# Neighbour lists from a dense adjacency: keys formed in SBUF by VectorE, or in PSUM by ScalarE and TensorE

## The chip, the cores and the metric

The kernel runs on one core of a Trainium2 chip. The core has five engines, each with a queue of its own that it works through in order: PE (TensorE, matrix products), DVE (VectorE), ACT (ScalarE), POOL (GpSimd) and SP, which here only starts transfers. They share SBUF; PE writes its products to PSUM[...], which DVE and ACT can also read and write. The time is device microseconds of one execution, the median of some runs; the profile is of one further execution. Line numbers in the profile of the kernel before are those of its source.

## The reference

A stack of four graph layers on x (8 x 2048 x 64), all masked by one 2048 x 2048 adjacency of zeros and ones with 8249 ones. The rows are uneven: the densest has 91, most have only a few. Cut to what matters here:

```
h = relu(layernorm(x));  x = x + softmax(where(adj > 0, h h^T / 8, -1e12)) h          # layer 0
h = relu(layernorm(x));  x = x + elu(softmax(where(adj > 0, lrelu(f1 + f2), -9e15)) hW) # layer 1
h = relu(layernorm(x));  x = x + layernorm(attention of 4 heads and of their output)    # layer 2, mask adj + I
h = relu(layernorm(x));  x = x + relu(softmax(where(adj > 0, lrelu(f1 + f2), -1e12)) hW) # layer 3
```

A row without any edge gets the mean over all nodes, which is why every layer's table carries one extra row, the column mean.

## The kernel before, in words

The 2048 nodes are 16 blocks of 128 rows, one row per partition; a node's row holds all eight batches, 512 values. Since the adjacency is sparse, the kernel doesn't compute 2048 x 2048 scores. It makes, once, a list of neighbours for each node, and every layer then gathers neighbour rows from a table in memory by indirect DMA (`gather`, L259). Block i has `ROWS[i]` list columns that all its nodes use, and `PACKED[i]` columns in which longer lists of different nodes are packed together, with selection matrices `sel` and `selt` (128 x 128) that copy a query to its packed edges and sum them back.

The lists are made in `lists` (L621), from a block's 128 x 2048 adjacency rows in int32, loaded by `load_adj` in one transfer of 1 MB, two buffers. In order:

- L626, DVE: key = (a > 0) * (2049 - column), in place in the tile `a`, read afterwards as float32. `keyrow` holds 2049 - column for all partitions.
- L632: the row is cut into segments, narrow at the left where the columns are dense, wide at the right; in each, MAX8 takes the eight largest keys into the candidate tile `c`. `SEGS` gives 8 segments and one round for blocks 2 to 15, 16 and one for block 1, 24 and two for block 0. Where there are two rounds, MATCH_REPLACE8 (L634) zeroes the eight found, in place, before the second MAX8.
- L642 and L644: of the candidates, the largest 16 (blocks 4 to 15), 24 (1 to 3) or 128 (block 0), again by MAX8 and MATCH_REPLACE8 in turn.
- L646 to L708: indices, masks, degrees, a running sum of degrees by a triangle matmul on PE (L661), the selection matrices (ACT L678, DVE L679, PE transposes L684, ACT L685), and the packed columns' indices (PE L696, DVE L698 to L708).

L637, L646 and L665 record whether a segment, a list or the packed columns overflowed. If one did, a flag makes a dense version of the whole stack run behind; the last lines of `edge_stack` compute that flag.

`pipeline` (L218) runs its stages over the blocks in the order of `MAKING` (15, 14, 13, 0, 12, 11, 10, 1, ...), each stage one block behind the stage ahead of it. Two pipelines make up this part (L710 to L712). The first normalizes x for layer 0: DVE sums (L276, L288), ACT squares (L290), DVE sums (L296, L297), POOL takes the power -1/2 (L299, L301), ACT scales (L307), SP stores the rows in the table, and POOL adds them up in `acc`; behind the last block PE sums `acc` over partitions (L371), DVE copies the mean row (L374) and SP stores it. The second runs load_adj, lists, gather, scores and exponents (`first0`), weighted sums (`second`), division and residual (`third0`), and the norm and table of layer 1, ending with that layer's mean row. Gathers of a layer can begin only when its whole table and mean row are stored.

The order of each engine's queue isn't written by hand. A scheduler takes the instructions of both pipelines, with their dependences, and puts each engine's into one fixed order when the kernel is built, by its own estimate of when each can start; tiles are handed out from pools with a fixed number of buffers. `ps_q` has three PSUM banks (tile `q`), used by the queries of the scores (L428, L437), the selection matrices and the transposes; `ps_m` and `ps_y` have two each, and one bank holds small tiles.

Of the kernel before, what the change touches and what calls it, by code (L numbers as in the profile page):

```python
# [7 lines left out]

F32 = mybir.dt.float32
F16 = mybir.dt.float16  # L10
I32 = mybir.dt.int32
U8 = mybir.dt.uint8
AF = mybir.ActivationFunctionType
OP = mybir.AluOpType
AX = mybir.AxisListType

P = 128
# [5 lines left out]
U16 = mybir.dt.uint16  # L23
# [6 lines left out]
PACKED = [8, 2, 3, 3, 2, 1, 2, 1, 1, 1, 1, 2, 2, 1, 1, 1]  # L30
WIDTH = [128, 24, 24, 24] + [16] * 12
SEGS = [(24, 2), (16, 1)] + [(8, 1)] * 14
RING = 26
TEMP = 16.0

# [11 lines left out]

def segments(n, count, least):

    ends, lo = [], 0  # L50
    for k in range(1, count + 1):
        hi = n * k * k // (count * count)
        if hi - lo >= least:
            ends.append((lo, hi))
            lo = hi
    if lo < n:
        ends[-1] = (ends[-1][0], n)
    return ends


# [1 line left out]
def edge_stack(ctx: ExitStack, tc: tile.TileContext, x_in, adj, w1, w1t, a1, wh, wht, bh, wo, bo,  # L62
# [9 lines left out]
    nc = tc.nc  # L72
    N, F = x_in.shape
# [13 lines left out]
    ident = const.tile([P, P], F32, name="ident")  # L87
# [15 lines left out]
    most2 = const.tile([P, NT], F32, name="most2")  # L103
    ring = const.tile([P, RING, F + B], F32, name="g")
    qidx = const.tile([P, sum(PACKED)], I32, name="qidx")
# [44 lines left out]
    with tc.tile_pool(name="setup", bufs=1) as sp, \  # L150
# [25 lines left out]
        for h in range(H):  # L176
            p = ps_w.tile([P, D], F32, name="p")
            nc.tensor.matmul(p, wh2[:, h].rearrange("d t c -> d (t c)"), wh2[:, h, 0, :],
                             start=True, stop=True)
# [57 lines left out]

    def rows(i, lo, hi, most=RING):

        t = lo  # L240
        while t < hi:
            at = (held[i] + t) % RING
            m = min(most, hi - t, RING - at)
            yield t, m, ring[:, at:at + m, :]
            t += m

    def row(i, t):
        return ring[:, (held[i] + t) % RING, :F]

    taken = {}  # L250

    def gather(k, i, st, behind=None):

        n = SLOTS[i]
        assert sum(SLOTS[j] for j in held) + n <= RING
        held[i], front[0] = front[0], (front[0] + n) % RING
# [332 lines left out]
    with tc.tile_pool(name="rows", bufs=2) as rp:  # L589
        rows_pool[0] = rp  # L590
        sel_all[0] = rp.tile([P, sum(PACKED) * P], F32, name="sel", bufs=1)
        with tc.tile_pool(name="lists", bufs=2) as pool, \
                tc.tile_pool(name="ps_q", bufs=3, space=bass.MemoryType.PSUM) as ps_q, \
                tc.tile_pool(name="ps_t", bufs=1, space=bass.MemoryType.PSUM) as ps_t:
            bank[0] = ps_t.tile([P, F], F32, name="tiny")
            keyrow = pool.tile([P, N], U16, name="keyrow", bufs=1)
            nc.gpsimd.iota(keyrow, pattern=[[-1, N]], base=N + 1, channel_multiplier=0,
                           allow_small_or_imprecise_dtypes=True)
            LS = 512
            iota = pool.tile([P, LS], F32, name="iota", bufs=1)  # L600
            nc.gpsimd.iota(iota, pattern=[[1, LS]], base=0, channel_multiplier=0,
                           allow_small_or_imprecise_dtypes=True)
# [3 lines left out]
                           allow_small_or_imprecise_dtypes=True)  # L606
            pe = pool.tile([P, NT], F32, name="pe", bufs=1)
            nc.gpsimd.iota(pe, pattern=[[P, NT]], base=0, channel_multiplier=1,
                           allow_small_or_imprecise_dtypes=True)
# [5 lines left out]
                                    pattern=[[1, P]], channel_multiplier=-1)  # L615

            def load_adj(i, st):
                st["a"] = pool.tile([P, N], I32, name="a")
                nc.sync.dma_start(out=st["a"], in_=adj[i * P:(i + 1) * P, :])

            def lists(i, st):  # L621

                K, T, W = ROWS[i], PACKED[i], WIDTH[i]
                E = T * P
                key = st["a"].bitcast(F32)
                nc.vector.scalar_tensor_tensor(key, st["a"], 0.0, keyrow, op0=OP.is_gt, op1=OP.mult)  # L626
                count, rounds = SEGS[i]
                segs = segments(N, count, 8 * rounds)
                c1 = pool.tile([P, len(segs), rounds, 8], F32, name=f"c{i}" if i < 2 else "c", bufs=1)
                for s, (lo, hi) in enumerate(segs):  # L630
                    for r in range(rounds):
                        nc.vector.max(out=c1[:, s, r, :], in_=key[:, lo:hi])  # L632
                        if r < rounds - 1:
                            nc.vector.match_replace(out=key[:, lo:hi], in_to_replace=c1[:, s, r, :],  # L634
                                                    in_values=key[:, lo:hi], imm_value=0.0)
                full = [s for s, (lo, hi) in enumerate(segs) if hi - lo > 8 * rounds]
                nc.vector.tensor_reduce(over[:, i, 0:1], c1[:, full[0]:, rounds - 1, 7:8].rearrange("p s o -> p (s o)"),  # L637
                                        AX.X, OP.max)
# [2 lines left out]
                for r in range(W // 8):  # L641
                    nc.vector.max(out=ell[:, 8 * r:8 * r + 8], in_=flat)  # L642
                    if r < W // 8 - 1:
                        nc.vector.match_replace(out=flat, in_to_replace=ell[:, 8 * r:8 * r + 8], in_values=flat,  # L644
                                                imm_value=0.0)
# [3 lines left out]
                at = OFF[i]  # L649
# [22 lines left out]
                mine = sel_all[0][:, POFF[i] * P:POFF[i] * P + E]  # L672
                for e0 in range(0, E, LS):
                    n = min(LS, E - e0)
                    if e0:
                        nc.vector.tensor_scalar(nmid, nmid, float(LS), None, op0=OP.add)
                    p = ps_q.tile([P, F], F32, name="q")
                    nc.scalar.activation(p[:, :n], iota[:, :n], AF.Abs, bias=nmid)  # L678
                    nc.vector.tensor_scalar(mine[:, e0:e0 + n], p[:, :n], half, None, op0=OP.is_lt)  # L679
                for t0 in range(0, T, 4):  # L680
                    n = min(4, T - t0)
                    p = ps_q.tile([P, F], F32, name="q")
# [8 lines left out]
                for t0 in range(0, T, step):  # L691
                    n = min(step, T - t0)
# [6 lines left out]
                    for t in range(n):  # L699
                        eq = pool.tile([P, P], F32, name="eq")  # L700
                        nc.vector.scalar_tensor_tensor(eq[:, :V], iotaj[:, :V], col[:, t:t + 1], pv[:, t, :V],
                                                       op0=OP.is_equal, op1=OP.mult,
                                                       accum_out=ke[:, t0 + t:t0 + t + 1])
                    nc.vector.tensor_scalar(qidx[:, POFF[i] + t0:POFF[i] + t0 + n], pv[:, :, V + 1], -1.0, N + 1.0,
                                            op0=OP.mult, op1=OP.add)
# [3 lines left out]

            pipeline(xin_rows, lambda i, st: norm_a(st["x"], st, False), pre_b, pre_c(None), pre_d(0, None))  # L710
            pipeline(load_adj, lists, take0, both(first0, xin_rows), second, third0, pre_b, pre_c(u1),
                     pre_d(1, u1))  # L712

# [148 lines left out]
    with psum_pools()[0] as ps_q, psum_pools()[1] as ps_t, tc.tile_pool(name="rows2", bufs=2) as rp:  # L862
# [72 lines left out]
        p = ps_m.tile([P, F], F32, name="m")  # L935
        nc.tensor.transpose(p[:1, :P], v[:, 3:4], ident)
        lo = small.tile([1, 1], F32, name="lo", bufs=1)
# [466 lines left out]
def whole_stack(tc, t, out):  # L1404
    nc = tc.nc
    D = t["gamma"].shape[0]
    with tc.tile_pool(name="flag", bufs=1) as pool:
        flag = pool.tile([1, 1], I32, name="flag")
        edge_stack(tc, t["x"], t["adj"], t["w1"], t["w1t"], t["a1"], t["wh"], t["wht"], t["bh"], t["wo"],
                   t["bo"], t["gamma"], t["beta"], t["w3"], t["w3t"], t["a3"], out, flag)  # L1410
        bad = nc.values_load(flag, min_val=0, max_val=1)
        with tc.If(bad > 0):
            gnn_stack(tc, t["x"].rearrange("n (b d) -> n b d", d=D), t["adj"], t["w1"], t["a1"], t["wht"],
                      t["bh"], t["wo"], t["bo"], t["gamma"], t["beta"], t["w3"], t["a3"],
                      out.rearrange("n (b d) -> n b d", d=D))
# [36 lines left out]
```

## Time and profile before

| | us |
|---|---|
| median of 3 runs | 1659.34 (1657.62 to 1660.49) |
| the profiled execution, first to last instruction | 1660.9 |
| layer 0's mean row, PE's sum of it (L371) | 106.06 to 107.92 |
| layer 1's mean row copied by DVE (L374) | 401.86 |
| first gather of layer 1 issued | 404.64 |

| over the whole execution | busy us | share | instructions |
|---|---|---|---|
| PE | 1214.6 | 73% | 3771 |
| DVE | 1311.9 | 79% | 2674 |
| ACT | 741.6 | 45% | 2362 |
| POOL | 1151.1 | 69% | 903 |

| lines of the lists on DVE | instructions | busy us |
|---|---|---|
| L626, forming the keys, 128 x 2048 | 16 | 38.7 (2418 ns each) |
| L632, MAX8 on the segments | 172 | 51.1 |
| L634, MATCH_REPLACE8 on segments, with its loads | 44 | 5.5 |
| L642, MAX8 on candidates | 49 | 15.7 |
| L644, MATCH_REPLACE8 on candidates, with its loads | 66 | 13.8 |

The profiled execution's own time is its span, 1660.9 us, which agrees with the runs. Shares over the whole execution are averages over stages with different limits, so what a line of the lists costs is read from the first 400 us alone, and there from what else its engine could have done at that moment. A line's busy time counts overlapping neighbours of the same engine once each; two short DVE instructions in a row overlap by some 0.08 us.

### The profile page before, as it was taken

The numbers are of one execution on the slowest core, as the hardware profiler recorded it, in microseconds if no ns is written. First come the engines' busy times: TensorE is split into PE (matmuls) and PEld (weight loads), VectorE is DVE, ScalarE is ACT, GpSimd is POOL, SyncE is SP. The second block draws the span as 40 slices with busy tenths as digits, with TensorE's granted clock in tenths as the row PEclk, the third lists the DMA queues.
The fourth block names the chain that finished last, engine by engine and source line by source line (L and its number), as shares of the span: only waits on it lengthen the run. The fifth ranks groups of instructions, "written<-read, shape, count | busy, mean of one in ns | idle before, by whom it ended". The sixth has DMA issues, their size and how long they took to land. (4 is left out here: it accounts for less than half of the span.)

```text
span 1660.9 us, 15702 instructions
## 1 busy us (share of the span) xinstructions
PE 1214.6 (73%) x3771; PEld 606.7 (37%) x3771; DVE 1311.9 (79%) x2674; ACT 741.6 (45%) x2362; POOL 1151.1 (69%) x903
## 2 busy tenths in 40 slices
PE   0025576776789974599997999999576868846898
PEld 0012243343454541234343344443233424423555
DVE  5978999994669987799999799861179979954667
ACT  5851223443257783356632455554334445560011
POOL 5765866786764215899689889998277889656650
PEclk9998877986889997799999999999877978857899
DMA  5545554453776537656255345300273443126771
GB/s 167 181 163 179 171 191 164 140 193 125 213 256 231 183 157 271 233 180 222 92 202 184 123 142 188 138 13 13 102 259 121 146 127 114 64 77 198 228 213 63
DMA packets 85787, 266.94 MB, mean 161 GB/s; under 512 B 14627, under 2 KB 14659, under 8 KB 75446
## 3 DMA queue, kind: packets, MB, share of 16 engines
q0 software_dynamic: 37328, 141.05, 27.4%
q1 hardware_dynamic: 48358, 124.79, 21.0%
q8 instruction: 32, 0.52, 0.1%
q14 instruction: 69, 0.57, 0.1%
HBM read 208.74 MB, written 57.05 MB: 160 GB/s over the span
## 5 line engine op out<-in xcount | busy, mean ns | idle before, releaser
L259 POOL DMA_INDIRECT g<-table,idx x405 | 396.2, 978 | 222.4 <-issue 131.7
L782 POOL TENSOR_TENSOR wh<-g,w 128x1024 f32<-128x1024 f32 x162 | 307.3, 1917 | 30.0 <-PE y L797 27.9
L394 PE MATMUL y<-wg,ident 128*128 128x512 f32 x392 | 232.4, 720 | 74.4 <-POOL wg L389 67.8
L299 POOL TENSOR_TENSOR ln_r<-ln_q,mhalf 128x8 f32<-128x8 f32 x80 | 135.9, 1702 | 129.0 <-DVE ln_q L297 93.0
L769 DVE TENSOR_REDUCE s<-prod 128x32 f32<-128x2048 f32 x81 | 183.9, 2285 | 14.6 <-ACT w L771 14.4
L389 POOL TENSOR_TENSOR wg<-g,w 128x1024 f32<-128x1024 f32 (+1 forms) x91 | 160.0, 1767 | 39.7 <-ACT w L445 31.7
L797 PE MATMUL y<-wh,ident 128*128 128x512 f32 x320 | 154.3, 609 | 28.1 <-POOL wh L795 24.4
L394 PE MATMUL y<-wg,selt 128*128 128x512 f32 x256 | 142.7, 669 | 6.0 <-POOL wg L389 6.0
L394 PEld LDWEIGHTS y<-wg,ident 128*128 128x128 f32 x392 | 79.6, 223 | 160.4 <-POOL wg L389 82.8
L797 PE MATMUL y<-wh,selt 128*128 128x512 f32 x256 | 124.6, 613 | 10.4 <-POOL wh L782 10.4
L805 ACT ACTIVATE yn<-y,rec 128x64 f32<-128x64 f32 x512 | 110.7, 366 | 27.6 <-PE y L797 26.8
L765 DVE TENSOR_TENSOR prod<-q,g 128x2048 f32<-128x2048 f32 x49 | 111.4, 2274 | 5.2 <-ACT g L763 5.1
L389 DVE TENSOR_TENSOR wg<-g,tiny 128x1024 f32<-128x1024 f32 (+1 forms) x92 | 98.1, 1086 | 12.3 <-PE y L394 11.9
L451 DVE SCALAR_TENSOR_TENSOR zt<-m,bhc,att 128x512 f32<-128x512 f32 x64 | 47.2, 737 | 74.9 <-ACT att L450 74.8
L408 PE MATMUL m<-w,selt 128*128 128x8 f32 (+1 forms) x384 | 61.0, 262 | 54.0 <-ACT w L554 19.1
L408 PEld LDWEIGHTS m<-w,selt 128*128 128x128 f32 x384 | 63.7, 215 | 100.0 <-ACT w L554 26.6
L307 ACT ACTIVATE xh<-x,ln_r 128x64 f32<-128x64 f32 x256 | 88.2, 427 | 25.5 <-POOL ln_r L301 25.4
L797 PEld LDWEIGHTS y<-wh,ident 128*128 128x128 f32 x320 | 58.9, 193 | 104.1 <-issue 64.4
L763 ACT COPY g<-g 128x512 f32<-128x512 f32 x81 | 50.4, 622 | 98.6 <-DVE prod L765 92.6
L437 PE MATMUL q<-rows,sel 128*128 128x512 f32 x128 | 81.4, 739 | 15.4 <-DVE prod L431 8.0
L765 DVE TENSOR_TENSOR prod<-qe,g 128x2048 f32<-128x2048 f32 x32 | 73.0, 2281 | 15.6 <-DMA qe<-qtab,qidx 14.5
L315 PE MATMUL q<-ident,xh 128*128 128x128 f32 x192 | 51.3, 341 | 44.9 <-ACT xh L307 43.1
(208 smaller groups left out, 2593.9 us busy)
## 6 DMA issues: line engine op xcount, KB each, us to landing
qtab<-q SPq DMA_DIRECT2D x16, 1040.0 KB, 4.0
a<-in_adj_dram SPq DMA_DIRECT2D x16, 1024.0 KB, 7.2
q<-qtab SPq DMA_DIRECT2D x14, 1040.0 KB, 5.3
table<-xh SPq DMA_DIRECT2D x48, 256.0 KB, 2.0
rows<-table SPq DMA_DIRECT2D x48, 256.0 KB, 3.8
xs<-x SPq DMA_DIRECT2D x48, 256.0 KB, 2.1
x<-xs SPq DMA_DIRECT2D x48, 256.0 KB, 3.6
table<-xh SPq DMA_DIRECT2D x32, 260.0 KB, 2.4
```

The source lines that it names most:

```text
L259: g = nc.gpsimd.indirect_dma_start(out=ring[:, (held[i] + t) % RING, :cols], out_offset=None, in_=table[k][:, :], in_offset=bass.IndirectO ...
L299: nc.gpsimd.tensor_tensor(st["rstd"][:, 0, :], q, mhalf, op=OP.pow)
L307: nc.scalar.activation(dst[:, b * D:(b + 1) * D], st["src"][:, b * D:(b + 1) * D], func, bias=0.0 if st["less"] is None else r[:, 1, b:b + ...
L389: eng.tensor_tensor(wg[:, :m].rearrange("p t (b d) -> p t b d", b=B), g[:, :, :F].rearrange("p t (b d) -> p t b d", b=B), w[:, t0:t0 + m, ...
L394: nc.tensor.matmul(y, lhs(i, t), wg[:, t - t0, :], start=(t == 0 and own is None), stop=(t == n - 1))
L408: nc.tensor.matmul(p[:, :cols], selt(i, t), packed[:, t, :], start=(t == 0), stop=(t == T - 1))
L437: nc.tensor.matmul(qe, sel(i, t - K), q, start=True, stop=True)
L765: nc.vector.tensor_tensor(pr.rearrange("p (b h) d -> p b h d", h=H), q[:, :B * H * D].rearrange("p (b h d) -> p b h d", h=H, d=D), heads(g ...
L769: nc.vector.tensor_reduce(s[:, t - lo, :], pr, AX.X, OP.add)
L782: nc.gpsimd.tensor_tensor(wg, heads(row(i, t))[:, :, None, :].to_broadcast([P, B, 2, D]), w[:, :, 2 * k:2 * k + 2, None].to_broadcast([P, ...
L797: nc.tensor.matmul(st["ys"][j], lhs(i, t), wg[:, 4 * j:4 * j + 4], start=False, stop=(t == n - 1))
L805: nc.scalar.activation(yn[:, b, h, :], st["ys"][j][:, b, h, :], AF.Copy, scale=st["rec"][:, 4 * j + b, 2 * k + h:2 * k + h + 1])
```

## The change

The keys are no longer formed by DVE. `load_adj` loads the adjacency in two halves of 1024 columns, and ACT turns each into its sign in bfloat16 (0 or 1), in a tile `e` of its own with two buffers; the int32 halves share two buffers of half a row. In `lists` PE makes, for each 512 columns, key = 4096 * sign + (2049 - column) in one PSUM bank: a first matmul with 4096 times the identity (`lift`), and a second one that adds the column keys to all partitions from two rows, a multiple of 64 and a rest of at most 63, both exact in bfloat16 (`keys`, `every`). A column with an edge has a key over 4096, one without has 1 to 2048. MAX8 and MATCH_REPLACE8 read the bank, and one more DVE instruction per block takes 4096 from the candidates and clips at zero, after which they are what they were before. The banks are taken from `ps_q`, four per block.

No segment may cross a border of 512 columns, so `segments` moves the marks nearest to 512, 1024 and 1536 onto them: the last segments of blocks 2 to 15 are 224, 512 and 512 wide instead of 352, 416 and 480. The number of segments and the total width are unchanged.

```diff
+LIFT = 4096.0
 def segments(n, count, least):
+    marks = [n * k * k // (count * count) for k in range(1, count + 1)]
+    for at in range(512, n, 512):
+        near = min(range(count), key=lambda k: abs(marks[k] - at))
+        marks[near] = at
     ends, lo = [], 0
-    for k in range(1, count + 1):
-        hi = n * k * k // (count * count)
+    for hi in marks:
         if hi - lo >= least:
             ends.append((lo, hi))
             lo = hi
-    if lo < n:
-        ends[-1] = (ends[-1][0], n)
     return ends
...
-            keyrow = pool.tile([P, N], U16, name="keyrow", bufs=1)
-            nc.gpsimd.iota(keyrow, pattern=[[-1, N]], base=N + 1, channel_multiplier=0,
+            keys = pool.tile([33, N], BF16, name="keys", bufs=1)
+            nc.gpsimd.memset(keys, 0.0)
+            nc.gpsimd.iota(keys[0:1, :], pattern=[[-64, N // 64], [0, 64]], base=N, channel_multiplier=0,
                            allow_small_or_imprecise_dtypes=True)
+            nc.gpsimd.iota(keys[32:33, :], pattern=[[0, N // 64], [-1, 64]], base=1, channel_multiplier=0,
+                           allow_small_or_imprecise_dtypes=True)
+            every = pool.tile([33, P], BF16, name="every", bufs=1)
+            nc.gpsimd.memset(every, 1.0)
+            lift = pool.tile([P, P], BF16, name="lift", bufs=1)
+            nc.scalar.activation(lift, ident, AF.Copy, scale=LIFT)
...
             def load_adj(i, st):
-                st["a"] = pool.tile([P, N], I32, name="a")
-                nc.sync.dma_start(out=st["a"], in_=adj[i * P:(i + 1) * P, :])
+                st["e"] = pool.tile([P, N], BF16, name="e")
+                for c in range(0, N, N // 2):
+                    a = pool.tile([P, N // 2], I32, name="a")
+                    nc.sync.dma_start(out=a, in_=adj[i * P:(i + 1) * P, c:c + N // 2])
+                    nc.scalar.activation(st["e"][:, c:c + N // 2], a, AF.Sign)
...
-                key = st["a"].bitcast(F32)
-                nc.vector.scalar_tensor_tensor(key, st["a"], 0.0, keyrow, op0=OP.is_gt, op1=OP.mult)
                 count, rounds = SEGS[i]
                 segs = segments(N, count, 8 * rounds)
                 c1 = pool.tile([P, len(segs), rounds, 8], F32, name=f"c{i}" if i < 2 else "c", bufs=1)
-                for s, (lo, hi) in enumerate(segs):
-                    for r in range(rounds):
-                        nc.vector.max(out=c1[:, s, r, :], in_=key[:, lo:hi])
-                        if r < rounds - 1:
-                            nc.vector.match_replace(out=key[:, lo:hi], in_to_replace=c1[:, s, r, :],
-                                                    in_values=key[:, lo:hi], imm_value=0.0)
+                for c in range(0, N, F):
+                    key = ps_q.tile([P, F], F32, name="q")
+                    nc.tensor.matmul(key, lift, st["e"][:, c:c + F], start=True, stop=False)
+                    nc.tensor.matmul(key, every, keys[:, c:c + F], start=False, stop=True)
+                    for s, (lo, hi) in enumerate(segs):
+                        if not c <= lo < c + F:
+                            continue
+                        lo, hi = lo - c, hi - c
+                        for r in range(rounds):
+                            nc.vector.max(out=c1[:, s, r, :], in_=key[:, lo:hi])
+                            if r < rounds - 1:
+                                nc.vector.match_replace(out=key[:, lo:hi], in_to_replace=c1[:, s, r, :],
+                                                        in_values=key[:, lo:hi], imm_value=0.0)
+                ends = c1.rearrange("p s r k -> p (s r k)")
+                nc.vector.tensor_scalar(ends, ends, LIFT, 0.0, op0=OP.subtract, op1=OP.max)
```

More of the change, by code (lines that the diff above doesn't have):

```diff
@@ L9 @@
 F32 = mybir.dt.float32
-F16 = mybir.dt.float16
+BF16 = mybir.dt.bfloat16
 I32 = mybir.dt.int32
```

## The prediction, made before the changed kernel had run

> **What bounds it now.** The chain that ended last reaches back only to 1548 us, far behind the lists, so I took the busy slices first, then time by stretch, then the instructions around the stretch's border. The busy slices of the page (40 slices of 41.5 us):
>
> ```profile
> span 1660.9 us, 15702 instructions
> ...
> PE   0025576776789974599997999999576868846898
> ...
> DVE  5978999994669987799999799861179979954667
> ACT  5851223443257783356632455554334445560011
> ```
>
> Lists are made in slices 0 to 8. There DVE is full; ACT is full only in slice 1, and PE does nothing until slice 2. Why PE starts late, and who waits for it, is in the timeline (start, duration, instruction, idle before it and its releaser):
>
> ```profile
> 106.06 1.86 PE L371 MATMUL m<-acc,ones 128*1 128x512 f32 x2 [92.00 <-POOL acc L368]
> ```
>
> ```profile
> 107.96 0.68 DVE L374 COPY mr<-m 1x512 f32<-1x512 f32 x1 [6.41 <-PE m L371]
> ```
>
> PE, which takes its queue in order, waits 92 us for the column mean of the first table. So the stage has two parts: an opening up to 107 us, in which the 16 blocks are normalized, and a main part up to 394 us. Time by stretch (columns: stretch, length, busy PE, PEld, DVE, ACT, POOL, clock, DMA):
>
> ```profile
> 0.00:107.00 107.00, 4.43 (x14) 3.00 (x14) 82.22 (x274) 75.69 (x264) 68.31 (x83) 1.00 0.51 164
> 107.00:394.00 287.00, 189.94 (x592) 99.73 (x590) 268.64 (x826) 96.39 (x335) 211.60 (x157) 0.86 0.52 172
> ```
>
> The main part is DVE's: 268.6 of 287 us. The opening is a round through ACT, POOL and DVE with ACT longest: it starts at 18.35 us and ends at 104.6, is busy 75.7 us of these 86.3, and idle 10.6. DVE has room here, and the kernel fills it with lists. How much, by stretch, for the key-forming line 626 and then for all that touches the candidate tile c (MAX8, MATCH_REPLACE8 and the short reduces; DVE time is the third busy entry of the second pair):
>
> ```profile
> 0.00:107.00 107.00, 13.69 (x6) 1.00 0.51 164
> 107.00:394.00 287.00, 24.99 (x10) 0.86 0.52 172
> ```
>
> ```profile
> 0.00:107.00 107.00, 0.00 (x0) 0.00 (x0) 40.26 (x170) 1.00 0.51 164
> 107.00:394.00 287.00, 0.00 (x0) 0.00 (x0) 47.24 (x177) 0.86 0.52 172
> ```
>
> Of 38.7 us of key forming, 13.7 lie in the opening, and with them 40.3 us of list searching (blocks 15, 14, 13 and nearly all of block 0, the costly one with 24 segments in two rounds). The end of this stage is a true border: the gathers of the next layer wait for the mean row of its table (first one at 404.6 us), so a microsecond here is one at the end.
>
> [...] L431, which reads q in PSUM, takes 1209 ns for 1024 elements, L433, which reads SBUF, 1205. I take MAX8 in PSUM as in SBUF (643 ns for 480)[...]. [...] the built list still has one table load. [...] Nothing in this trace is bfloat16 on PE; its float32 matmuls of 512 take 720 (L394).
>
> **Part by part.** *Removed:* 16 key-forming instructions, 38.7 us of DVE. Only the main part's 25.0 are worth anything; the 13.7 in the opening lay beside ACT.
>
> *Moved:* this decides. MAX8 now reads what PE has written. In the built instruction lists PE forms block 15's four key tiles ahead of the mean's matmul, and block 14's only behind it, behind block 15's triangle matmul, transpose and list product. DVE copies the mean row (old L374) as its 102nd instruction, where it was the 235th: the searching for blocks 14, 13 and 0 has gone from before to after it. Block 15's own share, from the timeline, is 2.1 + 0.65 (eight MAX8) + 0.9 (the rest) = 3.7 us. So 40.3 - 3.7 = 36.6 us leave the cover of the opening for the part that DVE bounds.
>
> *Added on DVE:* 16 subtract-and-clip over the candidates. The like of it is the 48-wide L930 at 0.18, less its overlap of 0.08: fifteen in the main part, the 352-wide one 0.35, together 2.5 us. DVE's main part: -25.0 + 36.6 + 2.5 = +14 us.
>
> *Added on ACT:* two Signs per block. Ten blocks' worth or more run in the main part, where ACT is busy 96 of 287 us: no price by itself. [...] The third and fourth also wait for data: two half-row buffers, so their loads start when Signs 1 and 2 end; 1024 KB take 7.2 us to land and 256 KB 3.4, so some 4.5 for 512 KB: about 3 + 1 us. Against this the table load (1.28) is done before the data come, and most of the 10.6 us idle should go, since DVE answers ln_q at once and not behind a 2.3 us key instruction (one stall alone was 5.45 for ln_r). Opening: -10.6 + 4 + 5.7 - 1.3 = -2 us (from -6 to +4).
>
> *Added on PE:* 128 bfloat16 matmuls, some 120 in the main part[...]. It doesn't become the bound, but it is in order. *Queues:* SP issues 32 half loads for 16; each waits for a Sign, and table stores and x loads stand behind it. Covered in the main part by the early load; its price in the opening is in the 4 us above. POOL gets two one-row iotas for one (1.89 us at 5 us, in cover).
>
> *The new wait:* the first MAX8 of a block waits for PE, and behind it in DVE's queue stand the scores of earlier blocks, for which ACT's exponents and POOL's weighting wait. Before, DVE's waits in the main part were few:
>
> ```profile
> DVE mr L374 <- PE m L371: 6.4, 1, 6.4
> DVE prod L439 <- DMA g<-table,idx: 4.2, 2, 3.7
> DVE ln_q L296 <- ACT ln_sq L284: 3.0, 2, 2.4
> DVE a L626 <- DMA a<-in_adj_dram: 2.9, 4, 1.5
> ```
>
> The 2.9 for adjacency go. For block 14 the first tile is two matmuls behind the list product[...]. Where PE stands at a weighted row (L394 waited 51 us for POOL) it can be more; where scores fill in, nothing. I take +6 net, from -6 to +25.
>
> Sum: -2 + 14 + 6 = +18 us on the profiled 1660.9, thus 1679. This execution lies 1.6 above the median of 1659.3; against the median it is 1677. The later layers keep their instructions, with small changes of order; I give them 3 us either way.
>
> **Rivals.** *The removal counts in full* (faster): if DVE finds list work in the opening after all, or the opening shortens to its ACT time (-6), the 15 us of waits after 108 us vanish [...], then -6 + 14 - 12 is -4: 1655. For it: ACT's 10.6 us idle. Against: the order of PE's queue is fixed when the kernel is built. It decides from a saving of 14 us in opening and waits. *It comes out even:* the same with half of these savings, 1656 to 1663. *PE sets the pace of the lists* (much slower): every key tile late by a weighted row, 2 us for fifteen blocks[...]: 1677 + 24, about 1701. For it: three PSUM buffers shared with scores and selectors, all held by block 0's two rounds. Against: PE has 97 us of slack in the main part. *The change doesn't do what it says:* a segment with eight edges would raise the flag and run the dense path behind. In the adjacency that the seed gives, blocks 2 to 15 have at most five per new segment, block 0 ten of sixteen: excluded.
>
> **Numbers.** Moved list work, 1677: 0.60, with its own range 1664 to 1692. PE's pace: 0.20. Even: 0.10. Faster: 0.10. Range: from 1660 (leaving out the faster case) to 1702. Faster by over 0.2% 0.10, within 0.2% 0.10, slower 0.80; 0.2%, 3.3 us, is about what a measurement of this kernel can tell from no change.
>
> **What would show it.** In the changed profile: the mean's matmul between 100 and 110 us; DVE busy some 45 us in the opening instead of 82; the second mean row's copy 10 to 30 us later than 401.9; no key-forming line, MAX8 of 512 near 0.68 us; DVE waits for PE's key tiles of about 10 us together. I am wrong if DVE's searching for blocks 14, 13 and 0 is found ahead of the mean's matmul, if MAX8 in PSUM runs at another rate, or if DVE's idle time in the main part is below 10 us or above 45.

## The result, and the profile after

The changed kernel takes 1723.1 us (median of 4 runs, 1719.9 to 1724.0), the kernel before 1659.9 beside it: a ratio of 1.037, with a 95% interval of 1.034 to 1.039. That is slower, as forecast, but by 63 us where 18 were forecast, and outside the range. The profiled execution has a span of 1718.1 us against 1660.9.

The busy slices of the changed kernel (40 slices, now of 43.0 us):

```profile
span 1718.1 us, 16030 instructions
...
PE   1042687788689987279998799999846778755897
...
DVE  3359978888457997699999789981148989973677
ACT  5951233443325788246653254555524535561101
```

DVE's first two slices stand at 3 and 3, where they stood at 5 and 9. The timeline of the changed kernel (PE, then DVE; start, duration, instruction, idle before it and its releaser) gives the two borders:

```profile
102.21 1.87 PE L373 MATMUL m<-acc,ones 128*1 128x512 f32 x2 [70.88 <-POOL acc L370]
```

```profile
104.12 0.68 DVE L376 COPY mr<-m 1x512 f32<-1x512 f32 x1 [9.72 <-PE m L373]
...
456.78 0.68 DVE L376 COPY mr<-m 1x512 f32<-1x512 f32 x1 [10.62 <-PE m L373]
```

The opening ends 3.9 us earlier, and the mean row of layer 1 comes 54.9 us later than the 401.86 of before. So 54.9 of the 57.2 us of span are lost by the end of the list stage, all of them in its main part. Busy time by stretch (stretch, length, busy PE, PEld, DVE, ACT, POOL, clock, DMA), and below it DVE's time on the candidate tile c:

```profile
0.00:103.00 103.00, 8.49 (x21) 3.82 (x22) 34.06 (x102) 80.98 (x269) 63.19 (x86) 1.00 0.48 149
103.00:446.00 343.00, 249.28 (x704) 117.58 (x702) 296.60 (x998) 121.82 (x356) 197.64 (x155) 0.75 0.47 150
```

```profile
0.00:103.00 103.00, 0.00 (x0) 0.00 (x0) 4.06 (x14) 1.00 0.48 149
103.00:446.00 343.00, 0.00 (x0) 0.00 (x0) 89.60 (x349) 0.75 0.47 150
```

The main part grew from 287 to 343 us. Half of the 56 is DVE's work (268.6 to 296.6, 28 us), half is time in which DVE stood idle (18.4 to 46.4, 28 us). Over the whole stage DVE has 20.2 us less to do than before (350.9 to 330.7) and stands idle 72 us longer, 44 of them in the opening. What DVE waits for in the main part (total us, times, longest us; L649 is MAX8 on a key tile, L680 the triangle matmul, L439 a query of the scores, L715 the list product):

```profile
DVE c L649 <- PE q L643: 16.1, 15, 2.7
DVE mr L376 <- PE m L373: 9.7, 1, 9.7
DVE st L682 <- PE m L680: 6.9, 14, 1.8
DVE prod L441 <- PE q L439: 4.9, 9, 1.4
DVE prod L433 <- ACT q L430: 4.3, 8, 0.6
DVE col L717 <- PE m L715: 2.6, 6, 0.5
```

Nearly all are waits for PE, where before they were few. (Of the 9.7 us at the mean row only 1.1 lie in the main part: it is the first mean, at 104.12.) PE's own waits there have a row of the same kind in the other direction:

```profile
PE m L680 <- DVE st L678: 39.9, 10, 24.4
```

The two engines wait for each other, but the 24.4 us are not where DVE loses. PE stands there for the list of block 0, from 142.45 to 166.80 us, and DVE is busy for 23.1 us of it, nearly all with that list. The run e10 below, in which PE forms no key, has the same wait, and it is longer:

```profile
PE m L661 <- DVE st L659: 43.9, 3, 39.6
```

What makes DVE wait for key tiles stands elsewhere in PE's queue. Ten of the fifteen waits, 14.9 of the 16.1 us, come where the key matmuls (L642, L643) stand behind the matmuls of weighted rows (L396). The longest, PE and then DVE:

```profile
351.94 3.76 PE L396 MATMUL y<-wg,ident 128*128 128x512 f32 x4
355.49 0.63 PE L642 MATMUL q<-e,lift 128*128 128x512 bf16 x1
356.06 0.60 PE L643 MATMUL q<-keys,every 33*128 33x512 bf16 x1
```

```profile
356.70 0.70 DVE L649 MAX8 c<-q 128x8 f32<-128x512 f32 x1 [2.72 <-PE q L643]
```

At the triangle DVE waits 14 times, 0.5 us on average, for the exchange itself; before, this exchange cost it no wait.

### The profile page after: what moved, and what is told of

Read it like the earlier page. It is cut to its first block, busy times and chain, and to the rows that moved or that the text cites. A ratio compares the mean times of both kernels' runs of the same rounds, so it can differ in the third digit from the quotient of the medians.

```text
span 1718.1 us, 16030 instructions
## 1 busy us (share of the span) xinstructions
PE 1280.4 (75%) x3899; PEld 624.2 (36%) x3899; DVE 1297.9 (76%) x2674; ACT 775.3 (45%) x2395; POOL 1135.1 (66%) x906
## 5 line engine op out<-in xcount | busy, mean ns | idle before, releaser
L261 POOL DMA_INDIRECT g<-table,idx x405 | 390.2, 963 | 243.8 <-issue 130.8
L396 PE MATMUL y<-wg,ident 128*128 128x512 f32 x392 | 238.8, 740 | 47.2 <-POOL wg L391 35.0
L301 POOL TENSOR_TENSOR ln_r<-ln_q,mhalf 128x8 f32<-128x8 f32 x80 | 132.2, 1656 | 154.8 <-DVE ln_q L299 95.8
L391 POOL TENSOR_TENSOR wg<-g,w 128x1024 f32<-128x1024 f32 (+1 forms) x91 | 155.0, 1713 | 56.6 <-PE y L396 13.4
L396 PE MATMUL y<-wg,selt 128*128 128x512 f32 x256 | 142.1, 668 | 7.5 <-POOL wg L391 7.5
L396 PEld LDWEIGHTS y<-wg,ident 128*128 128x128 f32 x392 | 82.3, 230 | 134.2 <-issue 69.1
L439 PE MATMUL q<-rows,sel 128*128 128x512 f32 x128 | 90.9, 823 | 12.8 <-DVE prod L433 4.4
L410 PE MATMUL m<-w,selt 128*128 128x8 f32 (+1 forms) x384 | 60.4, 260 | 35.6 <-ACT w L556 13.1
L309 ACT ACTIVATE xh<-ln_xc,ln_r 128x64 f32<-128x64 f32 x256 | 65.2, 335 | 43.8 <-POOL ln_r L301 23.5
L808 PE MATMUL y<-rows,ident 128*128 128x512 f32 x128 | 70.5, 637 | 17.8 <-DMA rows<-table 12.6
```

What stands on the lines that cost most here:

```text
L261: g = nc.gpsimd.indirect_dma_start(out=ring[:, (held[i] + t) % RING, :cols], out_offset=None, in_=table[k][:, :], in_offset=bass.IndirectO ...
L301: nc.gpsimd.tensor_tensor(st["rstd"][:, 0, :], q, mhalf, op=OP.pow)
L309: nc.scalar.activation(dst[:, b * D:(b + 1) * D], st["src"][:, b * D:(b + 1) * D], func, bias=0.0 if st["less"] is None else r[:, 1, b:b + ...
L391: eng.tensor_tensor(wg[:, :m].rearrange("p t (b d) -> p t b d", b=B), g[:, :, :F].rearrange("p t (b d) -> p t b d", b=B), w[:, t0:t0 + m, ...
L396: nc.tensor.matmul(y, lhs(i, t), wg[:, t - t0, :], start=(t == 0 and own is None), stop=(t == n - 1))
L410: nc.tensor.matmul(p[:, :cols], selt(i, t), packed[:, t, :], start=(t == 0), stop=(t == T - 1))
```

## The experiments

They ran on other chips than the result. There the kernel before takes 1703 to 1707 us, and e9 shows where the difference lies: its mean row of layer 1 comes at 402.2 us, against 401.9, so the list stage is the same and the later layers are longer. Times in the expectations are for the first chip; ratios to the kernel before, and the time of that mean row, can be compared directly. "Idle" is DVE's, in the opening and in the main part up to about 10 us ahead of the mean row, worked out from the busy time by stretch as above. Each row's stage times are from one profiled execution; that of e11 was the shortest of its four (1747 us against a median of 1759), that of e17 the longest (1738 against 1726). The two pairs of the same program (before and e9, changed and e5) agree within 0.3 and 2.4 us in the mean row. Another program is another matter: every edit makes the scheduler draw the order anew, and e14 to e17, which differ little in work, lie up to 18 us apart. A difference of that size can't be put to one cause.

| kernel | ratio, 95% interval | mean row of layer 1, us | DVE busy | idle, opening | idle, main |
|---|---|---|---|---|---|
| before (the result's run) | 1 | 401.9 | 350.9 | 24.8 | 18.4 |
| changed (the result's run) | 1.034 to 1.039 | 456.8 | 330.7 | 68.9 | 46.4 |
| e9 before, again | 0.998 to 1.000 | 402.2 | 351.3 | 26.7 | 16.1 |
| e5 changed, again | 1.029 to 1.038 | 459.2 | 332.1 | 69.5 | 46.5 |
| e4 keys formed twice in main | 1.027 to 1.035 | 437.8 | 385.4 | 21.5 | 22.1 |
| e10 before, lists held back | 1.038 to 1.044 | 453.0 | 364.2 | 60.7 | 19.2 |
| e1 four blocks' keys on DVE | 1.032 to 1.037 | 433.5 | 339.3 | 35.7 | 48.0 |
| e8 all keys on DVE, halves | 1.017 to 1.025 | 433.4 | 368.1 | 33.5 | 22.4 |
| e2 three lists ahead of mean | 1.030 to 1.033 | 447.6 | 326.3 | 67.9 | 42.8 |
| e12 mean tile apart | 1.040 to 1.049 | 453.5 | 330.9 | 62.4 | 51.7 |
| e6 before + unread matmuls | 1.024 to 1.032 | 425.7 | 353.4 | 36.6 | 27.0 |
| e7 keys twice on PE | 1.048 to 1.057 | 476.0 | 328.3 | 70.0 | 66.7 |
| e3 keys copied to SBUF | 1.055 to 1.060 | 488.0 | 327.1 | 70.2 | 80.7 |
| e11 e3, key tiles ahead | 1.029 to 1.035 | 430.3 | 322.1 | 68.3 | 30.6 |
| e13 e11, mean tile apart | 1.032 to 1.040 | 438.4 | 327.3 | 65.5 | 36.3 |
| e14 e11, four blocks on DVE | 1.005 to 1.011 | 405.2 | 336.2 | 27.8 | 32.0 |
| e15 e14, mean tile apart | 1.008 to 1.013 | 398.6 | 327.7 | 24.2 | 37.1 |
| e16 e15, five blocks | 1.011 to 1.017 | 416.2 | 329.7 | 24.3 | 53.0 |
| e17 e15, two sign tiles | 1.008 to 1.015 | 410.6 | 332.8 | 22.8 | 47.4 |

### First set: cover or round trips

Theory A: the loss is list searching that left the cover of the opening. Theory B: it is made by DVE's round trips to PE in the main part, because keys lie in PSUM banks that others need.

e1 gives blocks 15, 14, 13 and 0 back to DVE:

```diff
+                if i in HEAD:
+                    st["k"] = []
+                    for c in range(0, N, N // 2):
+                        a = pool.tile([P, N // 2], I32, name="a")
+                        nc.sync.dma_start(out=a, in_=adj[i * P:(i + 1) * P, c:c + N // 2])
+                        st["k"].append(a.bitcast(F32))
+                        nc.vector.scalar_tensor_tensor(a.bitcast(F32), a, 0.0, keyrow, op0=OP.is_gt, op1=OP.mult)
+                    return
```

> The changed kernel, but blocks 15, 14, 13 and 0 get their keys from DVE in SBUF again (two halves of 1024 each, one short subtraction more per block); the other 12 blocks keep ACT and PE. Theory A (most of the loss is list searching that lost the cover of the opening): the opening holds the searching of these four blocks again, the mean row of layer 1 is copied at 385 to 405 us instead of 457, and the time is 1640 to 1670 us. Theory B (the loss is made in the main part, by DVE's round trips to PE for its key tiles): 11 or 12 blocks still make them, so at least two thirds of the loss stays: 1700 us or more.

The opening filled again (idle 35.7 us instead of 69.5), and the mean row came 26 us earlier than in e5, at 433.5 and not at 385 to 405. The idle time of the main part stayed as it was, at 48.0. Some of the gain was lost again in the opening, whose mean is copied at 116.5 us (e5 104.4). So each theory has a part, and neither the whole. The layers behind took longer than with e5, so the ratio doesn't show the gain.

e2 writes the lists of three blocks ahead of the first mean:

```diff
+            ready = {}
+            for i in order[:3]:
+                load_adj(i, ready.setdefault(i, {}))
+                lists(i, ready[i])
+            mean_row(0)
```

> The changed kernel with the lists of blocks 15, 14 and 13 written ahead of the first mean row in the program, so that PE has their key tiles, triangle and list products ahead of the mean's matmul; every block still gets its keys from ACT and PE. Theory A: the searching of blocks 14 and 13 (some 15 us of DVE with its short instructions) lies in the opening, the time falls by 10 to 25 us against the changed kernel, to 1698 to 1713 us. Theory B: the same round trips are made, only earlier: 1715 us or more. If PE's queue delays the mean by more than the gain: above 1723 us.

At the mean row 11.5 us were gained on e5. DVE works 50.1 us in the opening instead of 34.0, but PE's queue now holds that mean behind three blocks' lists, and it is copied at 119.0 us instead of 104.4. This order alone doesn't give the cover back.

e3 frees the PSUM banks at once:

```diff
-                    key = ps_q.tile([P, F], F32, name="q")
...
+                    k = pool.tile([P, F], F32, name="key", bufs=5)
+                    nc.scalar.copy(k, p)
```

> The changed kernel, but ACT copies each key tile of 512 from PSUM to one of five SBUF tiles, a stage ahead, so that DVE holds no PSUM bank while it searches and needn't wait for the matmuls; the adjacency comes in quarters. The mean's matmul still stands ahead of block 14's key tiles. Theory A: the cover stays lost, 1700 to 1725 us. Theory B (banks and round trips): DVE's waits for key tiles (16 us) and most of the rest of the 32 us of new idle time go, 1675 to 1695 us.

Both were wrong: 488 us, far later than with the keys in PSUM. DVE's waits for key tiles fell only from 16 to 12 us, and its waits for other tiles of PE rose (waits of e3's DVE in the main part):

```profile
DVE col L722 <- PE m L720: 19.4, 16, 2.7
DVE st L687 <- PE m L685: 16.0, 12, 3.6
DVE rec L476 <- PE m L410: 13.3, 11, 5.3
DVE c L654 <- ACT key L637: 11.8, 20, 1.4
```

So freeing the banks didn't repair it, though ACT's copies are new work (158 us busy in the main part instead of 122). What is late is whatever DVE needs from PE, and that points to the order of PE's queue.

e4 doubles the key forming of 12 blocks in the kernel before (`for _ in range(2)` around the instruction).

> The kernel before, with the key forming of the 12 blocks other than 15, 14, 13 and 0 done twice (the second leaves the keys as they are): about 12 more instructions of 2.5 us, 30 us of DVE, nearly all in the main part. If DVE's work there counts one to one, as the prediction priced it: 1685 to 1692 us. If the stage has another bound beside DVE: under 1675 us.

DVE has 34.1 us more to do than in e9, and the mean row comes 35.6 us later: one to one, as the prediction priced it. The ratio is above the forecast because of the later layers.

### Second set: PE's load

Theory C: PE's added matmuls, in its queue and with the lower clock (0.75 in the main part, 0.86 before), are the cost. Theory D: it is not the load but that DVE depends on tiles which PE makes in the order of its queue.

e5 is the changed kernel once more.

> The changed kernel itself, once more beside the three others of this set, for its stage on the same chip. Every theory expects a ratio near 1.037 to before, and the mean row of layer 1 some 55 us later than with the kernel before.

It came out as expected. e6 adds PE's work to the kernel before, but nothing reads it:

```diff
+                for c in range(0, N, F):
+                    idle = ps_q.tile([P, F], F32, name="q")
+                    nc.tensor.matmul(idle, lift, bits[:, c % (2 * F):c % (2 * F) + F], start=True, stop=False)
+                    nc.tensor.matmul(idle, lift, bits[:, c % (2 * F):c % (2 * F) + F], start=False, stop=True)
```

> The kernel before, whose keys stay with DVE, with the two bfloat16 matmuls of 512 per key tile added on PE (8 per block) into tiles of ps_q that nothing reads. Theory C (PE's added work, its place in PE's queue and the lower clock granted with it are what costs): the mean row of layer 1 comes 25 us or more later than before, and the time rises by 1.5 to 3.5%. Theory D (it isn't PE's load, but that DVE now depends on tiles that PE makes in the order of its queue, so that list searching can't be placed where DVE is free): at most 10 us later, under 0.8%.

e7 doubles the matmuls of the changed kernel (`for _ in range(2)` around both).

> The changed kernel, with both matmuls of each key tile done twice (128 matmuls more, some 40 us of PE in all, 34 in the main part; the second pair starts the sum anew). Theory C: 30 us or more later than the changed kernel, ratio near 1.055. Theory D: DVE's wait for a key tile grows by the second pair, 0.7 to 1 us for each of 64 tiles at most and mostly hidden: 0 to 12 us later, ratio 1.037 to 1.045.

e6 comes 23.5 us later than e9, e7 16.8 later than e5: nearly theory C's numbers in e6, between the two in e7, where PE is busy 43.6 us longer than in e5, 39.4 of them in the main part. (e6's second matmul has 128 rows where the change has 33.) So one dose of key matmuls went with 17 to 24 us. That this is PE's load is not shown: e6's unread tiles also take `ps_q` banks from the scores, 5.2 of its 23.5 us lie in the opening, where PE has next to nothing to do, and a new order alone moves the stage by as much as 18 us. A lower clock needn't come from these matmuls either: e10, which has none, was granted 0.76 in its main part (e9 0.82, the changed kernel 0.75). e6 was granted 0.81 there and 0.58 in its opening, where all others have 1.00; why stays open.

e8 leaves all keys to DVE, but keeps segments, half loads and subtraction; its diff is e1's with all 16 blocks in HEAD, and a second subtraction for the far half.

> The changed kernel's segments, half loads of the adjacency and subtraction, but the keys of all 16 blocks formed by DVE in SBUF, in halves of 1024 (with one short subtraction more per block); no Sign, no key matmul. Both theories put the loss on ACT's and PE's part and expect about the kernel before plus 16 to 32 short instructions of 0.16 to 0.19 us: ratio 1.000 to 1.006. If the segments or the half loads are the cause: above 1.015.

It missed: 31 us later at the mean row, and a ratio above the 1.015 from which segments or half loads were to be the cause. It doesn't settle that, for the experiment is not clean. DVE has 16.8 us more to do than in e9: forming keys in halves takes 46.3 us instead of 38.7, the two subtractions 9.0 and 8.2 us, a mean of 564 and 511 ns instead of the 160 to 190 assumed (see the last section). It also waits 14.9 us for the adjacency, where two half-row buffers hold one block and not two. e1 bears some of this in its four blocks.

### Third set: each cause alone

e9 is the kernel before; e10 is the kernel before with one short instruction and one operand changed, so that DVE can't form any keys but block 15's until the sum behind the first mean is finished (96.84 us). PE and ACT do the work that they did.

```diff
+            gate = pool.tile([P, 1], F32, name="gate", bufs=1)
+            nc.vector.tensor_scalar(gate, acc[:, :1], 0.0, None, op0=OP.mult)
...
-                nc.vector.scalar_tensor_tensor(key, st["a"], 0.0, keyrow, op0=OP.is_gt, op1=OP.mult)
+                nc.vector.scalar_tensor_tensor(key, st["a"], 0.0 if i == order[0] else gate, keyrow, op0=OP.is_gt, op1=OP.mult)
```

> The kernel before itself, for its stage on the same chip as the three others of this set. Every theory expects a ratio of 1.00, the mean row of layer 1 at 402 to 406 us and DVE busy some 351 us up to there.

> The kernel before, where the key forming of every block but 15 compares with a zero that DVE takes from the finished sum of layer 0's rows, so that no list work but block 15's can lie in the opening; nothing else is changed, PE and ACT have no more work than before. If the loss of the cover costs what it holds (theory A): the searching of blocks 14, 13 and 0 and their key forming, some 36 plus 10 us, come on top of the main part, less 0 to 5 us of a shorter opening: mean row of layer 1 at 437 to 450 us, ratio 1.020 to 1.029. If the main part had room for it: under 415 us, ratio under 1.007.

Time by stretch, e9 and then e10:

```profile
0.00:109.50 109.50, 4.39 (x14) 3.00 (x14) 82.82 (x274) 75.79 (x264) 65.80 (x83) 1.00 0.50 160
109.50:394.00 284.50, 196.64 (x592) 105.34 (x590) 268.43 (x826) 96.63 (x335) 211.72 (x157) 0.82 0.53 174
```

```profile
0.00:100.70 100.70, 5.88 (x16) 3.50 (x16) 40.03 (x105) 74.97 (x262) 60.60 (x83) 1.00 0.46 144
100.70:444.00 343.30, 196.35 (x582) 103.36 (x582) 324.14 (x997) 94.99 (x332) 208.96 (x156) 0.76 0.47 153
```

The lost cover alone costs 50.8 us at the mean row, a little more than theory A's 35 to 48, and its ratio of 1.041 is as bad as the whole change. DVE does 42.8 us less in the opening and 55.7 more in the main part. Of the 55.7, the tile c accounts for 34.0 (47.2 to 81.2) and the key forming for about 12.5; some 9 us more are other instructions, nearly all of them the same ones, that take longer: the short ones of the TENSOR_SCALAR kind (see the last section). The main part's idle time hardly moves (16.1 to 19.2): without key tiles from PE, DVE hardly waits for PE there (13.2 us are waits for the adjacency).

e11 is e3 with one empty stage, `pipeline(load_adj, lambda i, st: None, lists, ...)`. In the built order PE then forms the next block's key tiles ahead of this block's triangle matmul.

> The kernel of e3_sbuf (key tiles copied to SBUF by ACT) with one empty stage between the loading and the lists, so that PE's queue holds the next block's key tiles ahead of this block's triangle matmul; the work is the same, only the order differs. Theory D (DVE and PE wait for each other through PE's queue): the 81 us in which DVE is idle in e3's main part fall below 55, and the mean row of layer 1 comes 20 to 40 us earlier than its 488 us. Theory C (PE's and ACT's added work): 480 us or more.

Time by stretch in the main part, e3 and then e11:

```profile
104.00:478.00 374.00, 247.84 (x704) 114.38 (x702) 293.30 (x997) 158.12 (x444) 197.75 (x155) 0.76 0.46 142
```

```profile
106.50:421.00 314.50, 234.38 (x697) 113.71 (x702) 283.91 (x976) 151.37 (x445) 198.02 (x156) 0.81 0.52 168
```

The same work, in another order, ends 57.7 us earlier than e3, and 28.9 earlier than e5; DVE's idle time falls from 80.7 to 30.6. Of the waits shown for e3, the first two are 3.4 and 1.5 us now. The empty stage also shifts gathers and scores against the lists, so it isn't proved that the key tiles' place alone does it; that the order does is.

e12 gives the mean its own PSUM tile in the changed kernel:

```diff
-                p = ps_m.tile([P, F], F32, name="m")
+                p = ps_y.tile([P, F], F32, name="y")
                 nc.tensor.matmul(p[:1, :], ones, acc, start=True, stop=True)
```

> The changed kernel, with the PSUM tile of the mean row from ps_y instead of ps_m, so that block 15's triangle matmul and block 14's key tiles go to PE ahead of the mean; the lists of blocks 13 and 0 still lie behind it in the built order. Theory A: DVE's work in the opening grows from 34 us to about 44, and the mean row of layer 1 comes 5 to 12 us earlier than with the changed kernel. Theory C or a mean delayed by the longer queue: no earlier.

DVE's work in the opening grew to 42.1 us, and the mean row came 5.7 us earlier than e5's: theory A's numbers, at their lower end, though 5.7 us is no more than a new order can do. The whole was slower than e5 all the same, in the later layers. So the mean's tile, handed out ahead of the triangle's from the same pool, kept block 14's lists behind the mean, but blocks 13 and 0 have other reasons to come late.

### Fourth set: both repaired

> The kernel of e11_sbuf_ahead with the mean row's PSUM tile from ps_y, so that the triangle matmuls of blocks 15 and 14 and the key tiles up to half of block 13's stand ahead of the mean on PE. If the opening's cover and the waits of the main part are separate parts: DVE's work in the opening grows by 10 to 15 us and the mean row of layer 1 comes that much earlier than e11's 430, at 415 to 422 us. If PE's longer queue delays the first mean by as much: 428 us or later.

e13 (e11 with e12's edit) missed: DVE's work in the opening grew by 3.3 us only, and the mean row came 8 us later than e11's.

e14 is e11 with the keys of blocks 15, 14, 13 and 0 from DVE, in quarters of 512, and three sign tiles instead of four; e15 adds e12's edit.

```diff
+                        k = pool.tile([P, F], F32, name="key", bufs=5)
+                        a = k.bitcast(I32)
+                        nc.sync.dma_start(out=a, in_=adj[i * P:(i + 1) * P, c:c + F])
+                        nc.vector.scalar_tensor_tensor(k, a, LIFT - c, keyrow, op0=OP.mult, op1=OP.add)
```

> Key tiles of blocks 15, 14, 13 and 0 made by DVE in SBUF in quarters of 512 (the adjacency times a constant plus a row of ramps, one instruction each; it takes the adjacency to hold 0 and 1 alone, as it does), those of the other 12 by ACT and PE, copied to SBUF and ordered ahead as in e11_sbuf_ahead. If the parts are separate, both are repaired: DVE busy some 80 us in the opening, its idle time in the main part about 30 us as in e11, the mean row of layer 1 at 385 to 405 us against before's 402, and a ratio of 0.99 to 1.01. If the main part loses again what the opening gains: 425 us or later, ratio 1.015 or more.

> The same with the mean row's PSUM tile from ps_y as well, so that the tails of the lists of the first blocks (triangle, transposes, products) can also go ahead of the mean. If parts are separate: as e14 or up to 10 us earlier. If the tails ahead of the mean delay it: 5 to 10 us later than e14.

Time by stretch in e15:

```profile
0.00:109.50 109.50, 12.10 (x34) 7.09 (x35) 85.26 (x349) 81.65 (x282) 64.65 (x87) 1.00 0.51 157
109.50:389.00 279.50, 212.35 (x667) 103.46 (x665) 242.40 (x767) 139.12 (x415) 198.31 (x156) 0.84 0.57 178
```

e14's mean row comes at 405.2 us, e15's at 398.6: 25 and 32 us ahead of e11's. The opening's idle time is that of the kernel before, the main part's that of e11 within 7 us, and e15's DVE has 24 us less to do than e9's. So both parts of the loss can be repaired in one kernel, and this brings the stage to 3.6 us ahead of before, in the best of four orders; e14 and the two runs below end it 3 to 14 us later than before. The whole is still 1.0% slower: the later layers take 8 us more by the profiled runs (1316 against 1308), and some 19 by the medians (15 in all, and the 3.6 gained before).

e16 and e17 change one size of e15 each (five blocks with DVE; `bufs=2` for the sign tiles), to see whether this belongs to the repair.

> As e15_hybrid_ahead_apart, with block 12 too among the blocks whose keys DVE makes (five instead of four). The mean row of layer 1 at 395 to 410 us (2.6 us of key forming more, one block's round trips less). If the longer later layers belong to the repair: 1310 us or more from there to the end again, ratio 1.005 to 1.012. If they belong to the order drawn: anything from 1300 to 1330 us, ratio 0.995 to 1.02.

> As e15_hybrid_ahead_apart, with two tiles for the sign of the adjacency instead of three. Mean row of layer 1 at 397 to 408 us. If the longer later layers belong to the repair: 1310 us or more from there to the end, ratio 1.005 to 1.012. If they belong to the order drawn: 1300 to 1330 us, ratio 0.995 to 1.02.

They end the stage 18 and 12 us later than e15, with the opening filled in the same way and 47 to 53 us idle in the main part. So the cover is a stable gain, the waits in the main part are not: one block more or one buffer less redraws the order and moves them by 10 to 16 us. From the mean row to the end (profiled span less the mean row's time) e16 takes 1312 and e17 1326 us, e9 1308, e5 1302; e10, whose keys all come from DVE, takes 1326. No kernel here is faster than before, and what the later layers' 1302 to 1329 us depend on stays open: their instructions are the same, their order isn't.

## Why the prediction was wrong in size

Its direction and its place were right: list searching that leaves the cover of the opening for the part that DVE bounds. By its own steps:

- **Opening, -2 (from -6 to +4): right.** The mean's matmul came 3.9 us earlier. DVE was busy 34 us there; the 45 given as a sign doesn't follow from the prediction's own terms, 82.2 - 13.7 - 36.6 = 31.9. The 5.7 us for Signs in the sum were the author's estimate, which no trace of before shows; the six took 6.1 us (1.99 for two in a row). The third waited 3.2 us for its data (3 forecast), the fourth 0.2 (1 forecast), with half loads of 5.0 us against 4.5.
- **MAX8 in PSUM at the speed of SBUF: right.** 512 elements took 690 ns, against 643 for 480 in SBUF before; at the five widths that both kernels use in most blocks (32 to 288) MAX8 took 1 to 10 ns more, 452 against 442 for 288.
- **Moved list work, 36.6, and one to one: right in kind.** Tile c took 42.4 us more in the main part (47.2 to 89.6), where 36.6 and the subtraction's 2.5 were forecast. (The terms named for those 2.5 add up to 1.8; the fifteen subtractions took 4.0, the 352-wide one 0.35 of them.) e4 shows the rate, e10 the loss without PE.
- **DVE's main part, +14: failed, it was +28.** 3.3 of the missing 14 are on tile c. The other 10.6 are on everything outside c and key forming: 196.4 us became 207.0 (the busy times above, less those of c and of the removed line). These instructions don't take longer: their durations add up to 251.7 us before and 251.3 after, ten short list instructions that left the opening among them. What shrank is their overlap with their neighbours in DVE's queue. The prediction took each at its cost inside a full queue; that the new waits pull such neighbours apart is argued, not shown. e10's 9 us are of another kind, for there the durations grew (251.4 to 262.9).
- **New waits, +6 net (from -6 to +25): the step that failed most.** DVE's idle time in the main part rose by 28.0. Its waits for key tiles were 16.1, where about 10 were forecast. The price, the author's estimate, which no trace of before shows, put the tile two matmuls behind the list product; in the run the late tiles stood behind weighted rows, up to 2.72 us at once, which the prediction names ("it can be more") and puts no number to. And it counted only this new wait. Older exchanges came to cost as well: the triangle 6.9 us where there had been none, the list product 2.6 instead of 0.4, the scores 4.9 instead of 1.9, and 4.3 for queries that ACT copies.
- **PE "doesn't become the bound but is in order", at no price beside the wait: not borne out.** The key matmuls kept PE busy 51 us in the main part. e6 and e7 came 17 to 24 us later with one dose of these matmuls; how much of it is PE's load stays open.
- **The rival "PE sets the pace of the lists", 1701, at 0.20** had the mechanism of the late key tiles right, a weighted row ahead of them: 30 us estimated, 14.9 measured. Its other reason, shared PSUM buffers, isn't supported: e3 freed them and lost time. The 24 of its sum are the 30 less the 6 already counted.
- The condition stated for being wrong, DVE idle over 45 us in the main part, is met with 46.4.

The sum of the main part, as measured: 28 of work and 28 of idle time against 14 and 6 forecast. Those 36 us, with 2 less in the opening, 3 more up to the mean row's copy and 2 behind it, make the 39 by which the profiled span missed its 1679; the medians add 7, as they lie 46 apart.

## What to carry to other kernels

Work that one engine does in the cover of another is worth its full price the moment a new dependence takes it out (in e10 DVE did 42.8 us less in the opening, and the stage ended 50.8 us later), and a new dependence can do that by the order in which tiles are handed out alone. When data that an engine used to make for itself come from a second in-order queue, price every exchange between the two queues, not just the new one, and look at what stands ahead of the new producer in its queue: an order that forms the tiles one block earlier was worth 58 us here against the same work without it (e3), and 29 against the changed kernel. The early blocks, which ran in cover, are better kept on the old way: with that, e14 to e17 ended the stage 14 to 32 us ahead of e11.

## What the runs showed of the hardware

Short DVE instructions of the TENSOR_SCALAR kind took up to some 30 times their usual 0.15 us. In the changed kernel a 128x2 one took 4.70 us (timelines of POOL and of DVE):

```profile
193.39 3.75 POOL L391 TENSOR_TENSOR wg<-g,w 128x1024 f32<-128x1024 f32 x2
197.11 1.25 POOL L370 TENSOR_TENSOR acc<-acc,xh 128x512 f32<-128x512 f32 x1
```

```profile
193.68 4.70 DVE L726 TENSOR_SCALAR idx<-ke 128x2 int32<-128x2 f32 x1
```

It begins 0.3 us after the first of three POOL instructions that follow each other closely, and ends at 198.38, with the last of them (198.36). The others there go the same way: in the list stages of the kernel before and the changed kernel, 30 TENSOR_SCALAR instructions of at most 64 columns (21 and 9) took over 0.6 us. Each of them began while POOL was busy and ended within 0.04 us of the end of a POOL instruction. No DVE instruction of another kind, of at most 64 columns, took over 0.45 us there. Why the two end together is not shown; no run took POOL's work away. So 16 or 32 "short" instructions of this kind are not priced by their median: e8's subtractions took a mean of 564 and 511 ns.

The bfloat16 key matmuls of 512 columns, whose two weights of 128 and of 33 rows alternate, started 0.52 to 0.55 us apart when block 14's tiles were formed at 106 us, and 0.31 to 0.33 at 175 us, with a granted clock of 1.00 both times. What makes the two rates is not shown.
